# A later second batch of gates in six units, and out_proj's rows added by TensorE in the last unit but one

## The chip, the cores and the metric

The kernel runs on one core of one Trainium2 chip. The metric is the device time of one execution in microseconds; the median of several runs is given. In the profile, PE is TensorE (its matmuls; PEld its weight loads), DVE is VectorE, ACT is ScalarE, POOL is GpSimd and SP is SyncE, which issues the DMAs.

## The reference

The input x has 4 batches of 1024 tokens of 256 channels; all arithmetic is float32. Cut to what matters:

```python
h = layernorm(x)                                         # layer 1: Mamba block, gated MLP
z, xi, B, C, dt_raw = split(rmsnorm(h) @ in_proj.T)      # widths 256, 64, 64, 256, 128
dt = softplus(dt_raw @ dt_proj.T + dt_bias)              # 256 channels, 32 states each
for each token:                                          # the selective scan
    state = exp(dt * A) * state + (dt * xi) * B
    y = sum over states(state * C)
h = h + ((y + xi * D) * silu(z)) @ out_proj.T
hn = rmsnorm(h)
x = x + h + (silu(hn @ gate.T) * (hn @ up.T)) @ down.T   # inner width 704
xn = layernorm(x)                                        # layer 2
out = x + fwht(silu(xn @ W1.T) * (xn @ W3.T)) @ W2.T     # inner width 1024; the kernel folds
                                                         # the Walsh-Hadamard transform into W2
```

## The kernel before

**Units.** The work is cut into eight units, `us[0]` to `us[7]`: four batches by two halves of 512 tokens. A unit's second half starts from the state that its first half left. The scan of a unit runs as 16 steps `q`, 128 in all; one step holds 128 lanes of (channel, state) by 4 blocks by 512 tokens.

**Ticks.** The order of the work on every engine is written out by hand. `at(tick, lane, fn)` puts a piece of work into a list, and a loop at the end of the kernel goes through the ticks, two for each `q`, 256 for the scans, and issues in each tick: lane `PE`, lane `ACT`, the product `times_b` on DVE (L838, tile bx), lane `ACTb` (the copy of B into the PSUM tile pb, L825), the two exps of the next q on ACT (L808), a scan on DVE (L847), lane `DVE`, the second scan, `POOL0`, every second tick the product with C on POOL (`times_c`, L860, in place in da), lane `POOL`, every other tick the sum over states on PE (`sum_states`, L871, into py, after a first matmul with xr and dd, L869, where a half of the unit begins), lanes `PEend`, `ACTend`, SP and the loads. An engine takes its instructions in the order in which they are issued, so the lane and tick of a piece decide behind what it stands. Nothing else plans the order; semaphores between engines are put in by the framework.

**Post-work.** While unit k+1 is scanned, what follows unit k's scan is done in between, from tick E = 32k + 32 on; `post()` puts it into the lists:

- `hr`: the normalized input rows (ACT), and out_proj's product added to them (`add_rows`).
- `row_stats` (ACT, L193 and L196), a few small POOL instructions (`small2`), `hn` (ACT, L226), its transposes (PE, L239) and copies (`ht`, ACT, L246).
- gate and up: `gated()` issues for two batches of three chunks the products pg and pu on PE (L252, two per tick), silus (L289) and ups (L296) on ACT, the products m on POOL (L300). It also carries a half of z of the unit two later (silu at L486). pg and pu are in PSUM tiles of a pool of four, "dense".
- `down`: four row blocks of 128 tokens (`add_rows`, L338), the two copies into hr, `row_stats`, `small3`, `hn`, transposes, `xt`.
- w1 and w3: three batches of `gated()`; then W2's four row blocks, stored at the end.

`add_rows` has three ways to add rows to hr. In way "pe" a matmul with the identity puts hr's rows into PSUM first (L336), the products are added there (L338), and ACT copies the sum back over hr (L352). In way "pool" ACT copies the product out (ev, L360) and POOL adds it (L364). Without a way DVE adds it from PSUM (L348).

The units have three kinds of due times. `many` are units 0 to 5. `us[-2]` is unit 6 (E = 224), whose post-work lies beside the last unit's scans. `last` is unit 7 (E = 256), whose post-work comes after all scans; no scan stands beside it. Half a unit's steps share one pb: its copy is due on ACT at tick E + 15 (and E + 31), and bx of the next tick reads it.

For the prediction's steps in the units 0 to 5: the first batch of gates starts at E + 11, the second at E + 14; the down rows are due at E + 19, 20, 21 and 22 in lane `PE`, that is ahead of the tick's sum over states; yt, the copy of the finished half sum py (L889, ACT), comes at E + 18 or 19, and after it POOL multiplies it by zs (L892). xr·dd of the next half writes py again.

Of the kernel before, what the change touches and what calls it, by code (L numbers as in the profile page):

```python
# [27 lines left out]
def tile_block(ctx: ExitStack, tc: tile.TileContext, a, out):  # L28
# [41 lines left out]
    def dense_psum():  # L70
        return ps_m.tile([P, T], F32, tag="dense", name="dense")
# [148 lines left out]
    def rsqrt_eps(dst, var):  # L220
        nc.gpsimd.tensor_scalar(dst, var, EPS, 1.0, ALU.add, ALU.mult)
        nc.gpsimd.tensor_tensor(dst, dst, mhalf, ALU.pow)

    def scaled_rows(dst, src, scale, bias, ts):
        for t in ts:
            nc.scalar.activation(  # L226
                dst[:, t, :],
                src[:, t, :],
                AF.Identity,
                bias=bias[:, t : t + 1] if bias is not None else 0.0,  # L230
                scale=scale[:, t : t + 1],
            )
# [31 lines left out]
    def at(tick, lane, fn, *args):  # L264
        todo[tick][lane].append(partial(fn, *args))
# [54 lines left out]

            at(tick + 3, "POOL" if three or u is not us[-2] else "POOL0", product, i)

    def add_rows(ticks, u, lhs, rhs, lane="PE", way=None):


        po = {}

        def pe(t):
            if t % 2 == 0:
                po[t // 2] = dense_psum().rearrange("p (t d) -> p t d", t=2)  # L330
            left, right = lhs(), rhs()
            n = len(left)
            dst = po[t // 2][:, t % 2, :]
            if way == "pe":
                rows = u["hr"][:, t, :]
                nc.tensor.matmul(dst, lhsT=ident, rhs=rows, start=True, stop=False)  # L336
            for k in range(n):
                nc.tensor.matmul(  # L338
                    dst,
                    lhsT=left[k][:, t * P : (t + 1) * P],  # L340
                    rhs=right[k],
                    start=(k == 0 and way != "pe"),
                    stop=(k == n - 1),
                )

        def add(i):
            hr = u["hr"][:, 2 * i : 2 * i + 2, :]
            nc.vector.tensor_tensor(hr, hr, po[i], ALU.add)  # L348

        def replace(i):  # L350
            copy = nc.vector.tensor_copy if by_vector(i) else nc.scalar.copy
            copy(u["hr"][:, 2 * i : 2 * i + 2, :], po[i])  # L352

        def by_vector(i):
            return u is us[-1] and i

        def evict(i):
            ev = p3.tile([P, T], F32, tag="up", name="ev")
            po[i] = ev.rearrange("p (t d) -> p t d", t=2), po[i]
            nc.scalar.copy(*po[i])  # L360

        def add_pool(i):
            hr = u["hr"][:, 2 * i : 2 * i + 2, :]
            nc.gpsimd.tensor_tensor(hr, hr, po[i][0], ALU.add)  # L364

        for t in range(TT):
            at(ticks[t], lane, pe, t)
            if t % 2:
                after = ticks[t] + 1
                if way == "pe":  # L370
                    at(after, "DVE" if by_vector(t // 2) else "ACTend", replace, t // 2)
                elif way == "pool":
                    at(after, "ACTend", evict, t // 2)
                    at(after + 1, "POOL", add_pool, t // 2)
                else:
                    at(after, "DVE", add, t // 2)
# [270 lines left out]
    def post(u, E, other):  # L647


        s = {}  # L650
        last = u is us[-1]

        many = us.index(u) < len(us) - 2

        def hr(ts):
            if 0 in ts:
                u["hr"] = p2.tile([P, TT, DM], F32, tag="hr", name="hr")
            scaled_rows(u["hr"], u["x"], u["r1"], u["nm1"], ts)

        def small2():  # L660
            t = sm.tile([P, 2, TT], F32, tag="s2", name="s2")
            r3 = t[:, 1, :]
            rsqrt_eps(r3, u["mv"][:, 1, :])
            s["r3"] = r3

        def small3():
            t = sm.tile([P, 2, TT], F32, tag="s2", name="s2")
            nm, r4 = t[:, 0, :], t[:, 1, :]
            nm16, var = u["mv"][:, 0, :], u["mv"][:, 1, :]
            rsqrt_eps(r4, var)  # L670
            nc.gpsimd.tensor_tensor(nm, nm16, r4, ALU.mult)
            nc.gpsimd.tensor_scalar(nm, nm, 16.0, None, ALU.mult)
            s["r4"], s["nm"] = r4, nm

        def hn(scale, bias):
            s["tok"] = p1.tile([P, TT, DM], F32, tag="tok", name="hn")
            scaled_rows(s["tok"], u["hr"], s[scale], s[bias] if bias else None, range(TT))

        def big(name):
            if last:  # L680

                k = NQ + (1 if name == "m" else 3)
                tiles = [das[i % 5] for i in (k, k + 1)]
                u[name] = [tiles[c // 4][:, c % 4, :] for c in range(8)]
            else:
                tile = p1.tile([P, 8, T], F32, tag="big", name=name)
                u[name] = [tile[:, c, :] for c in range(8)]

        def store(lo=0, n=TT):
            b, first = u["b"], u["c"] * T + lo * P  # L690
            nc.sync.dma_start(
                out=out[b, first : first + n * P, :].rearrange("(t p) d -> p t d", p=P),
                in_=u["hr"][:, lo : lo + n, :],
            )

        at(E + 3, "ACT", hr, (0, 1))
        at(E + 4, "ACT", hr, (2, 3))
        add_rows(
            (E + 3,) * TT,
            u,  # L700
            lambda: [u["yt"][:, k, :] for k in range(2)],
            lambda: [W["wo"][:, k, :] for k in range(2)],
            "PEend",
            way="pool" if many else None,
        )
        for i in range(2):
            at(E + (5 + i if many else 4), "ACTend", row_stats, u, "hr", (2 * i, 2 * i + 1), False)

        F = E + 1 if many else E - 2
        at(E + 7 if many else E + 5, "POOL", small2)  # L710
        at(F + 8, "ACT", hn, "r3", None)
        at(F + 9, "PE", lambda: transposes(u, s["tok"]))
        at(F + 9, "ACTend", transposed, u, "ht")
        at(F + 9, "POOL", lambda: nc.gpsimd.tensor_tensor(u["hr"], u["hr"], u["x"], ALU.add))
        at(F + 10, "PE", big, "m")
        sizes = [min(P, DFF - c * P) for c in range(6)]
        chunks = list(enumerate(sizes))
        for i in range(2):
            gated(F + 10 + 3 * i, u, "m", "wg", "wu", chunks[3 * i : 3 * i + 3], "ht",
                  (other, i) if other else None)  # L720
        down = (18, 19, 20, 21) if many else (17, 17, 18, 18)
        add_rows(
            [F + t for t in down],
            u,
            lambda: [u["m"][c][:n] for c, n in enumerate(sizes)],
            lambda: [W["wd"][:n, c, :] for c, n in enumerate(sizes)],
            way="pe",
        )
        at(F + down[1] + 1, "ACTend", row_stats, u, "hr", (0, 1))
        if last:  # L730
            at(F + down[3] + 1, "DVE", row_stats_vector, u, "hr", (2, 3))
        else:
            at(F + down[3] + 1, "ACTend", row_stats, u, "hr", (2, 3))
        at(F + down[3] + 2, "POOL", small3)
        if not many:
            F -= 3
        at(F + 24, "ACTend" if many else "ACT", hn, "r4", "nm")
        at(F + 25, "PE", lambda: transposes(u, s["tok"]))
        at(F + 25, "ACTend", transposed, u, "xt")
        at(F + 26, "PE", big, "g")  # L740
        chunks8 = [(c, P) for c in range(8)]
        for i in range(3):
            gated(F + 26 + 3 * i, u, "g", "w1", "w3", chunks8[3 * i : 3 * i + 3], "xt")

        o2 = (E + 31, E + 36, E + 50, E + 50) if not (many or last) else range(F + 36, F + 40)
        add_rows(
            o2,
            u,
            lambda: u["g"],
            lambda: [w2h[:, c, :] for c in range(8)],  # L750
            way=None if last else "pool",
        )
        if last:
            at(o2[1] + 1, "SPend", store, 0, 2)
            at(o2[3] + 1, "SPend", store, 2, 2)
        else:
            at(o2[3] + 6, "SPend", store)
# [142 lines left out]
    for k, u in enumerate(us):  # L900
        post(u, 32 * k + 32, us[k + 2] if k + 2 < len(us) else None)
# [148 lines left out]
```

## Time and profile before

| | |
|---|---|
| runs | 1125.77, 1126.01, 1127.81 us; median 1126.01 |
| profiled execution | 1129.06 us, of which the span of the profile is 1127.3 |
| mean granted TensorE clock | 0.925 |
| scans (bx of tick 0 to the last scan's end) | to 1022.8 us of the span |
| bx of tick E + 16, E = 64 / 96 / 128 / 160 / 192 | starts at 335.5 / 459.6 / 582.3 / 707.3 / 831.3 us |

The page cuts the span into 40 slices of 28.2 us; each digit is a tenth of the slice:

```profile
PE   7656246979999799989998999979998999898998
DVE  4899799999989999899999999899989989894000
ACT  3956456887869796888779796979777777584331
POOL 6767668878998899888988899878988788685222
PEclk9777558989999899989999899989999999898999
```

From the ninth slice on, PE and DVE both stand at eight or nine tenths; the last three slices, without DVE, are the post-work of the last unit. `PEclk` is the granted clock; in nearly every unit it loses a tenth or two in one slice.

In the lines of a timeline the columns are start and busy time in us, engine, line, operation, output and inputs, shape, count; in square brackets how long the engine was idle just before, and whom it waited for. In a list of waits the columns are the total, the times and the longest.

### The profile page before, as it was taken

Reading aid. Unit: us, or ns where it says so; the run is one execution under the profiler, and the core shown is the slowest. Engines: PE = TensorE matmul, PEld = TensorE weight load, DVE = VectorE, ACT = ScalarE, POOL = GpSimd, SP = SyncE. Lnnn points to the kernel's source line nnn. Section 1 sums busy time; section 2 is a strip of 40 time slices with the busy share of each in tenths; the row PEclk is TensorE's granted clock in tenths of the full one; section 3 lists DMA queues with packets and bytes.
Section 4 is the critical chain, followed back from the end, with each engine's and each line's share of the span. In section 5 each row is a group of like instructions: output and inputs, shape, how many; then the busy total and the mean of one; then the engine's idle time right before and its main releaser. Section 6 shows DMA issues by size and latency. Waiting matters only on the chain.

```text
span 1127.3 us, 12518 instructions
## 1 busy us (share of the span) xinstructions
PE 980.5 (87%) x3470; PEld 474.4 (42%) x3470; DVE 943.9 (84%) x813; ACT 805.0 (71%) x1443; POOL 882.8 (78%) x512
## 2 busy tenths in 40 slices
PE   7656246979999799989998999979998999898998
PEld 3121012333644345443644354433644363434555
DVE  4899799999989999899999999899989989894000
ACT  3956456887869796888779796979777777584331
POOL 6767668878998899888988899878988788685222
PEclk9777558989999899989999899989999999898999
DMA  7999998998998989998998989899999978760000
GB/s 236 375 363 347 319 377 313 327 317 309 306 342 298 351 302 316 320 333 300 319 347 309 343 284 338 307 337 310 314 321 323 325 255 315 264 223 1 1 19 19
DMA packets 108390, 321.94 MB, mean 286 GB/s; under 512 B 11488, under 2 KB 22176, under 8 KB 108320
## 3 DMA queue, kind: packets, MB, share of 16 engines
q1 hardware_dynamic: 106464, 318.39, 80.8%
q10 hardware_dynamic: 1856, 2.75, 0.7%
q8 instruction: 28, 0.46, 0.2%
q14 instruction: 42, 0.34, 0.1%
HBM read 302.22 MB, written 18.87 MB: 285 GB/s over the span
## 4 chain that ended last, share of the span: by engine, by line
PE 44%; ACT 12%; DMA 7%; DVE 5%; POOL 4%; issue 4%; SPq 0%; DVEq 0%; ACTq 0%; POOLq 0%
PE dense L252 27%; PE dense L338 11%; ACT da L808 5%; DMA da<-dtd 4%; PE py L871 4%; DVE da L847 3%; POOL da L860 3%; DMA ub<-ud 2%; DVE bx L838 2%; ACT up L296 1%; ACT un L226 1%; ACT hr L226 1%; PE dense L336 1%; ACT junk L196 1%; ACT junk L193 1%
## 5 line engine op out<-in xcount | busy, mean ns | idle before, releaser
L860 POOL TENSOR_TENSOR da<-da,cr 128x2048 f32<-128x2048 f32 x128 | 579.2, 4526 | 41.4 <-DVE da L847 19.1
L808 ACT ACTIVATE da<-da,nega 128x512 f32<-128x512 f32 x508 | 335.7, 715 | 72.9 <-DMA da<-dtd 67.3
L838 DVE TENSOR_TENSOR bx<-ub,pb 128x1024 f32<-128x1024 f32 x254 | 312.2, 1229 | 28.5 <-ACT pb L825 11.7
L847 DVE TENSOR_TENSOR_SCAN da<-da,carry,bx 128x512 f32<-128x512 f32 x256 | 313.9, 1267 | 22.0 <-ACT da L808 6.1
L847 DVE TENSOR_TENSOR_SCAN da<-da,bx 128x512 f32<-128x512 f32 x256 | 298.5, 1207 | 17.0 <-DVE bx L838 3.0
L252 PE MATMUL dense<-xt,w 128*128 128x512 f32 x512 | 241.8, 626 | 7.9 <-ACT xt L246 7.9
L871 PE MATMUL py<-da,rsel 128*32 128x512 f32 x1024 | 155.7, 670 | 83.7 <-POOL da L860 83.7
L252 PEld LDWEIGHTS dense<-xt,w 128*128 128x128 f32 x512 | 99.1, 200 | 146.9 <-issue 114.2
L296 ACT COPY up<-dense 128x512 f32<-128x512 f32 x112 | 63.4, 578 | 56.5 <-PE dense L252 56.3
L338 PE MATMUL dense<-w2h,g 128*128 128x256 f32 x448 | 102.1, 383 | 1.2 <-ACT ut L246 1.2
L871 PEld LDWEIGHTS py<-da,rsel 128*32 128x32 f32 x1024 | 23.8, 112 | 179.0 <-POOL da L860 118.4
L338 PEld LDWEIGHTS dense<-w2h,g 128*128 128x128 f32 x448 | 83.5, 190 | 24.2 <-issue 10.4
L300 POOL TENSOR_TENSOR g<-si,up 128x512 f32<-128x512 f32 x56 | 71.0, 1274 | 28.1 <-ACT up L296 28.1
L252 PE MATMUL dense<-ut,win 128*128 128x512 f32 x192 | 92.7, 614 | 0.2 <-ACT ut L246 0.2
L252 PE MATMUL dense<-ht,wg 128*128 128x512 f32 x192 | 87.6, 600 | 3.0 <-ACT ht L246 3.0
L338 PE MATMUL dense<-wd,m 128*128 128x256 f32 x336 | 85.7, 397 | 3.3 <-POOL m L300 3.3
L289 ACT ACTIVATE si<-dense 128x512 f32<-128x512 f32 x112 | 61.9, 595 | 34.9 <-PE dense L252 34.5
L252 PE MATMUL dense<-ht,wu 128*128 128x512 f32 x160 | 73.9, 601 | 1.8 <-ACT si L289 1.8
L300 POOL TENSOR_TENSOR m<-si,up 128x512 f32<-128x512 f32 (+1 forms) x42 | 52.6, 1274 | 26.1 <-ACT up L296 26.1
L338 PEld LDWEIGHTS dense<-wd,m 128*128 128x128 f32 x336 | 63.2, 195 | 21.2 <-issue 9.3
L808 ACT ACT_TABLE_LOAD x46 | 59.0, 1283 | 0.8
L252 PEld LDWEIGHTS dense<-ut,win 128*128 128x128 f32 x192 | 36.8, 197 | 52.5 <-issue 41.0
(110 smaller groups left out, 884.4 us busy)
## 6 DMA issues: line engine op xcount, KB each, us to landing
da<-dtd SPq DMA_DIRECT2D x254, 512.0 KB
ub<-ud SPq DMA_DIRECT2D x254, 512.0 KB
cr<-cd SPq DMA_DIRECT2D x64, 256.0 KB
x<-in_x SPq DMA_DIRECT2D x8, 512.0 KB
dtd<-dt SPq DMA_DIRECT2D x16, 256.0 KB
ud<-du SPq DMA_DIRECT2D x16, 256.0 KB
cd<-cc SPq DMA_DIRECT2D x16, 256.0 KB
xr<-xbd SPq DMA_DIRECT2D x60, 64.0 KB
```

The lines of the kernel that those rows point to most:

```text
L193: nc.scalar.activation(junk, src[:, t, :], AF.Identity, scale=-1.0 / (16 * DM), accum_out=nm)
L226: nc.scalar.activation(dst[:, t, :], src[:, t, :], AF.Identity, bias=bias[:, t : t + 1] if bias is not None else 0.0, scale=scale[:, t : t ...
L252: nc.tensor.matmul(dst[:n], lhsT=w[:, k, col : col + n], rhs=src[:, k, :], start=(k == 0), stop=(k == 1),)
L289: nc.scalar.activation(g[i]["si"][:n], g[i]["pg"][:n], AF.Silu)
L296: nc.scalar.copy(g[i]["up"][:n], g[i]["pu"][:n])
L300: nc.gpsimd.tensor_tensor(u[dst][c][:n], g[i]["si"][:n], g[i]["up"][:n], ALU.mult)
L338: nc.tensor.matmul(dst, lhsT=left[k][:, t * P : (t + 1) * P], rhs=right[k], start=(k == 0 and way != "pe"), stop=(k == n - 1),)
L808: nc.scalar.activation(da, da if q else s["u"]["pdt", b], AF.Exp, scale=an[:, s["h"], s["j"], b, s["g"] : s["g"] + 1],)
L838: nc.vector.tensor_tensor(s["bx"], s["ub", b0 // 2], u["pb"].unsqueeze(1).broadcast_to([P, 2, T]), ALU.mult)
L847: nc.vector.tensor_tensor_scan(da, da, s["bx"][:, b % 2, :], start, ALU.mult, ALU.add)
L860: eng.tensor_tensor(da, da, s["cr"].unsqueeze(1).broadcast_to([P, n, T]), ALU.mult)
L871: nc.tensor.matmul(u["py"][32 * b : 32 * b + 32, :], lhsT=rsel[:, 2 * s["j"] + s["g"], :], rhs=s["da"][:, b, :], start=False, stop=last,)
```

## The change

For the six `many` units:

- the second batch of gates starts at E + 15 instead of E + 14;
- the down rows are due at E + 20, 21, 21, 22 in lane `PEend` (behind the tick's sum over states) instead of E + 19, 20, 21, 22 in lane `PE`;
- the copy of the first two row blocks into hr, and their statistics, come at E + 22 instead of E + 21; those of the last two stay at E + 23, and so does all that follows.

For `us[-2]`:

- all hr rows are made at E + 3; out_proj's rows are added in way "pe" (four identity matmuls, two copies on ACT) instead of by two adds on DVE; the statistics are at E + 4 and E + 5, small2 at E + 6;
- hn, ht, hr + x, gates and down come a tick later than before (gates at E + 9 and E + 12, down at E + 16, 16, 17, 17), the copies into hr, the statistics and small3 two ticks later (copies at E + 18 and E + 19, small3 at E + 20), and hn, xt and the w1/w3 batches two ticks later (E + 21, 22, and 23, 26, 29);
- W2's row blocks are at E + 36, 36, 50, 50 instead of 31, 36, 50, 50, so that all four stand behind the scans, which end at E + 32.

For `last` nothing changes. SP's instructions keep their order. On PE in the `many` units the pieces between pu of the first batch and the last down row stand as follows (sum n is the sum over states of tick E + n):

```
before: pg3 pg4 pg5 z | sum15 | pu3 pu4 c | sum17 | down0 | xr·dd sum19 | dt | down1 down2 | sum21 | c | down3 | sum23
after:  pg3 pg4 | sum15 | pg5 z c pu3 pu4 | sum17 | xr·dd sum19 | dt | down0 | sum21 | down1 down2 | c | down3 | sum23
```

On POOL the second batch's products m move behind the product with C of tick E + 18; on ACT the exps of tick E + 16 move ahead of the second batch's silus.

The diff, with the `add_rows` signature and its copies first:

```diff
-    def add_rows(ticks, u, lhs, rhs, lane="PE", way=None):
+    def add_rows(ticks, u, lhs, rhs, lane="PE", way=None, extra=0):
...
-                after = ticks[t] + 1
+                after = ticks[t] + 1 + extra
...
-        at(E + 4, "ACT", hr, (2, 3))
+        at(E + 4 if many else E + 3, "ACT", hr, (2, 3))
...
-            way="pool" if many else None,
+            way="pool" if many else None if last else "pe",
...
-            at(E + (5 + i if many else 4), "ACTend", row_stats, u, "hr", (2 * i, 2 * i + 1), False)
-
-        F = E + 1 if many else E - 2
-        at(E + 7 if many else E + 5, "POOL", small2)
+            at(E + (5 + i if many else 4 if last else 4 + i), "ACTend", row_stats, u, "hr", (2 * i, 2 * i + 1), False)
+
+        F = E + 1 if many else E - 2 if last else E - 1
+        at(E + 7 if many else E + 5 if last else E + 6, "POOL", small2)
...
-            gated(F + 10 + 3 * i, u, "m", "wg", "wu", chunks[3 * i : 3 * i + 3], "ht",
+            gated(F + 10 + (4 if many else 3) * i, u, "m", "wg", "wu", chunks[3 * i : 3 * i + 3], "ht",
...
-        down = (18, 19, 20, 21) if many else (17, 17, 18, 18)
+        extra = int(not (many or last))
+        down = (19, 20, 20, 21) if many else (17, 17, 18, 18)
...
+            "PEend" if many else "PE",
             way="pe",
+            extra=extra,
         )
-        at(F + down[1] + 1, "ACTend", row_stats, u, "hr", (0, 1))
+        at(F + down[1] + 1 + extra, "ACTend", row_stats, u, "hr", (0, 1))
...
-            at(F + down[3] + 1, "ACTend", row_stats, u, "hr", (2, 3))
-        at(F + down[3] + 2, "POOL", small3)
+            at(F + down[3] + 1 + extra, "ACTend", row_stats, u, "hr", (2, 3))
+        at(F + down[3] + 2 + extra, "POOL", small3)
         if not many:
-            F -= 3
+            F -= 3 - extra
...
-        o2 = (E + 31, E + 36, E + 50, E + 50) if not (many or last) else range(F + 36, F + 40)
+        o2 = (E + 36, E + 36, E + 50, E + 50) if not (many or last) else range(F + 36, F + 40)
```

## The prediction

> **What bounds the kernel now.** First the page's busy lines, then the waits by total, then VectorE (DVE) tick by tick, then TensorE (PE) around one unit's join.
>
> ```profile
> PE 980.5 (87%) x3470; PEld 474.4 (42%) x3470; DVE 943.9 (84%) x813; ACT 805.0 (71%) x1443; POOL 882.8 (78%) x512
> DVE bx L838 <- ACT pb L825: 11.7, 6, 3.5
> ```
>
> PE and DVE are both near full. DVE sets the tick: one bx of 1.23 and two scans of 1.2 to 1.27 make 3.7 to 3.9 us, 256 times. What DVE loses in the loop is therefore lost time. The second line (total, times, longest) is one such loss: bx of tick E+16 waits for the copy of B. By unit E=64 to 192 it is 3.48, 2.17, 1.51, 1.80 and 2.44 us. I follow E=128:
>
> ```profile
> 577.92 1.98 PE L252 MATMUL dense<-ht,wu 128*128 128x512 f32 x4
> 580.00 0.59 ACT L296 COPY up<-dense 128x512 f32<-128x512 f32 x1 [2.20 <-PE dense L252]
> 581.72 0.58 ACT L825 COPY pb<-br 128x512 f32<-128x512 f32 x1
> 582.33 1.23 DVE L838 TENSOR_TENSOR bx<-ub,pb 128x1024 f32<-128x1024 f32 x1 [1.51 <-ACT pb L825]
> ```
>
> Read upwards: bx waits for pb, which stands in ScalarE's (ACT's) queue behind the copy of up2, which waits 2.20 us for PE. So PE is late. How it came to be late shows in the windows after the unit's joins (columns: us, PE busy, granted clock, DMA share, GB/s):
>
> ```profile
> 617.50:620.90 3.40, 1.06 (x8) 1.00 0.82 290
> 620.90:631.20 10.30, 8.83 (x15) 0.50 1.02 396
> 631.20:707.00 75.80, 74.80 (x278) 1.00 0.93 315
> ```
>
> From 631.2 to 707.0, that is from the w1 gates to the next unit's tick E+16, PE is busy 74.80 of 75.80 us: whatever starts this stretch later makes the next bx at E+16 later, one for one. The stretch starts when the last down row (down3, ends 615.2) has been copied, its statistics taken, and hn made and transposed. **The many-unit cycle is TensorE's**: pu2, down3, hn, w1 gates, next pu2.
>
> **Units 0 to 5: what moves.** All that PE does up to pu2 keeps its order, so the stall at E+16 is not taken away at its source. Behind pu2 the orders are
>
> before: pg3 pg4 pg5 z, sum15, pu3 pu4 c, sum17, **down0**, xr·dd, sum19, dt, down1 down2, sum21, c, down3;
> after: pg3 pg4, sum15, pg5 z c pu3 pu4, sum17, xr·dd, sum19, dt, **down0**, sum21, down1 down2, c, down3.
>
> ```profile
> 593.04 1.06 PE L871 MATMUL py<-da,rsel 128*32 128x512 f32 x8
> 594.58 2.95 PE L338 MATMUL dense<-wd,m 128*128 128x256 f32 x12
> 597.45 1.12 PE L869 MATMUL py<-xr,dd 128*128 128x512 f32 x2
> 599.45 1.16 PE L871 MATMUL py<-da,rsel 128*32 128x512 f32 x8 [0.87 <-POOL da L860]
> 612.33 2.95 PE L338 MATMUL dense<-wd,m 128*128 128x256 f32 x12
> 595.66 0.57 ACT L889 COPY yt<-py 128x512 f32<-128x512 f32 x1
> 590.60 1.27 POOL L300 TENSOR_TENSOR m<-si,up 128x512 f32<-128x512 f32 x1 [3.68 <-ACT up L296]
> 594.87 4.53 POOL L860 TENSOR_TENSOR da<-da,cr 128x2048 f32<-128x2048 f32 x1
> ```
>
> Before, down0 (594.04 with its ident matmuls, to 597.45) fills the time in which ACT gets to the yt copy; xr·dd writes the PSUM tile that this copy reads. After, xr·dd comes first and waits. The added wait: sum17 still ends at 594.04 (the same instructions stand ahead of it, in another order), yt ends near 596.2 (ACT's work ahead of it, ups, cc and exps, is the same): 2.2 us. Queued behind it on PE: sum19, dt and every down row. Bounds of this wait from the rows: nothing, if ACT comes to yt 2.2 us earlier; 5.1 us, the longest PE wait on yt anywhere in the trace (unit 0). I take 2.2, worked out in place.
>
> Then, with row-to-row times: xr·dd 1.12 to 597.3, sum19 1.09 to 598.4, dt 1.82 to 600.2, down0 3.41 to 603.6. sum21 needs POOL's da of tick E+20. POOL after: da18 moves ahead of the products into POOL's idle 3.68 us: from 589.7 (its scans end) 4.8 with the carry copy to 594.5, three m of 1.27 to 598.3, yt·zs 1.28 to 599.6, da20 4.8 to 604.4. So sum21 waits 0.8 and ends 605.4; down1 and down2 6.72, c 1.82, down3 3.31: 617.25, against 615.21. In waits: 2.2 + 0.8 − 0.87 (sum19 waits no more), so **+2.0 us** for down3.
>
> What hides it: after down3 come copy (0.59), statistics (2.4), exps, hn. The exps of tick E+26 wait 1.24, 0.59 and 0.94 us for DMA in E=64, 128, 160, and a late ACT uses these up; E=96 and 192 have no such cover. The w1 gates move by 1.3 (E=32, where PE waits 4.53 for POOL at 246.3 anyway), 0.75, 2.05, 1.5, 1.05, 2.0: **+8.7 us**.
>
> At nothing: the first hr copy and its statistics a tick later (ACT is idle 1.24 before the second copy at 615.32; without that cover at most their 0.59 + 2.4); SP's queue, which keeps its order, so that transfers wait for the same or earlier sums (sum19 599.4 to 597.3, sum21 609.1 to 604.4), with a gain of at most the 0.57 us that the scan at 606.46 waits for its exp.
>
> **The granted clock.** In the row 617.50 PE is busy 31% of 3.4 us, and the next 10.3 us run at 0.50; windows with 48% or more kept 1.00. A new wait of 2.2 us inside one such stretch leaves some 35%, across two of them over half. So about half of the six units may fall, each losing 0.7 (one stretch, 0.8 of it covered by sum21's wait) to 2.4 us. Bounds 0 to 6 × 2.4 = +14; I take **+1.5**, as the rows right after (sum19, dt, down0) are the ones slowed, and one stretch busy over 88% brings the clock back.
>
> The Trainium skill, "TensorE: Matmul & The Clock Gate", section "HAM oscillation — how this bites in real kernels", speaks of no PE-idle gaps over about 3.4 us. By it a wait of 2.2 us would cost no clock, and the sum would be 1.5 us lower. The trace differs: a single wait of 2.69 us at 621.25, after 1.12 us of waiting, lies in the stretch that cost half the clock.
>
> **Unit 6 (E=224) and the tail.**
>
> ```profile
> 911.51 0.69 DVE L348 TENSOR_TENSOR hr<-hr,dense 128x512 f32<-128x512 f32 x1 [2.66 <-PE dense L338]
> 913.24 0.69 DVE L348 TENSOR_TENSOR hr<-hr,dense 128x512 f32<-128x512 f32 x1 [1.04 <-PE dense L338]
> 977.63 2.45 DVE L847 TENSOR_TENSOR_SCAN da<-da,carry,bx 128x512 f32<-128x512 f32 x2 [2.87 <-ACT da L808]
> 966.23 0.59 ACT L352 COPY hr<-dense 128x512 f32<-128x512 f32 x1 [8.38 <-PE dense L338]
> 1036.88 0.59 ACT L360 COPY ev<-dense 128x512 f32<-128x512 f32 x1 [1.61 <-PE dense L338]
> ```
>
> The two adds and their waits leave DVE: 2.66 + 0.69 + 1.04 + 0.69 = 5.1 us. The copies L352, which hold the exps behind them (8.38 us, then the scan's 2.87 and 0.38), come two ticks later, after their rows: 3.25 us. DVE gains 8.3. What is late next is PE: it takes on four ident matmuls (0.54 each by their starts, 2.2) and drops one W2 block (3.6) from the loop. Its own waits to the end go: 3.72 at 978.73, 2.30 and 1.30 for the last sums. −3.7 − 2.3 − 1.3 − 3.6 + 2.2 = −8.7 at best for the last sum (ends 1028.8 before); with 1.1 us of new waits for silu and ups at E+13, −7.6. The W2 block then stands in the tail between out_proj and hn of the last unit, as the present one does (1033.17 to 1036.8, its ev on ACT ahead of hn): +3.6. Net −5.1 to −4.0; bounds by rows: −8.3 if PE hides the block, and +2.2 if DVE's gain turns wholly into waits for PE while the four matmuls stay. I take **−4.7**.
>
> **Sum.** +8.7 + 1.5 − 4.7 = +5.5. The profiled execution took 1129.06 (span 1127.3), 3 us above the median of 1126.0; on that, 1131.5, on the profile 1134.5. I predict 1131.
>
> **The rivals.**
> A, forecast: the TensorE cycle is longer by the yt wait, 1130 to 1133. For: 74.80 of 75.80. Chance 0.53.
> B, faster: ACT reaches yt early, or POOL's earlier da pays back what PE waits (POOL loses its 3.68 us of idleness), so that the six units cost under 0.4 us each, and the eight us of DVE stalls in unit 6 decide: −4.7, 1121. For: POOL stands in PE's waits on sums (0.87, and 1.12 at 617.40). Against: those sums are before down3 only in part. It decides from less than 0.4 us a unit. Chance 0.21.
> C, balance: the DMA waits at E+26 hide more, 0.8 us a unit: 1126. Chance 0.13.
> D, clock: every unit's wait of 2.2 us costs a stretch at half clock, 1.5 us more in each: 1126 + 8.7 − 4.7 + 9 = 1139. Chance 0.13.
>
> **The numbers.** Within 0.2% (2.25 us, about what a measurement here tells from no change) is C; faster is B; slower A and D: 0.21, 0.13, 0.66. The range runs from 1119 (B with the unit-6 bound halfway) to 1139 (the middle of D); outside lie about half of D and a third of B's low side. The likeliest case alone is 1128 to 1134.
>
> **What would show it.** Right: PE waits of about 2.2 us at xr·dd on yt in each of six units; bx on pb from 11.7 to about 20; down3 ending 34.9 us after bx of E+16 instead of 32.9; unit 6's DVE adds and the 2.87 gone; two W2 blocks ahead of the last hn. Wrong: yt copied before sum17 ends; the pb wait at or below 11.7; new DVE waits in unit 6 over 3 us; a DMA wait that ends a tick where ACT did.

## The result, and the profile after

The changed kernel takes 1139.66 us (median of four runs, 1137.17 to 1140.95); the kernel before, 1126.91 in the same set (1125.77 to 1130.58). The ratio is 1.0105, 95% interval 1.0073 to 1.0137: slower by 8 to 15 us. The forecast was +5, to 1131, with a range to 1139: the sign is right, and the loss is a little over twice the forecast. In microseconds the median lies just above that range; the ratio on the 1126.0 from which the forecast started gives 1137.8. The profiled execution is the fastest of the four (1137.17, span 1135.4), 8.1 us above the profiled one of before, while the medians lie 12.8 apart: the two traces show some two thirds of the loss.

Where the time is: the start of bx (us of the span) at a few ticks, from the two traces.

| tick | before | after | difference |
|---|---|---|---|
| 64 (first of the third unit) | 272.3 | 272.8 | +0.5 |
| 128 | 521.1 | 522.7 | +1.6 |
| 160 | 642.4 | 648.5 | +6.1 |
| 224 (first of the last unit) | 890.8 | 901.0 | +10.2 |
| 255 (last) | 1019.0 | 1023.6 | +4.6 |
| transposes of the last unit's hn | 1037.9 | 1046.0 | +8.1 |

So the six units lost 10.2 us, unit 6 gave back 5.7 in the loop, and the tail took 3.5 again. TensorE's (PE's) timeline of the same unit as in the prediction (E = 128; bx of E + 16 now starts at 587.17; line numbers are three higher than before):

```profile
597.88 1.06 PE L874 MATMUL py<-da,rsel 128*32 128x512 f32 x8
601.60 1.92 PE L872 MATMUL py<-xr,dd 128*128 128x512 f32 x2 [2.66 <-ACT yt L892]
603.45 1.92 PE L874 MATMUL py<-da,rsel 128*32 128x512 f32 x8
605.29 1.98 PE L447 MATMUL dense<-raw,dtw 128*128 128x512 f32 x4
607.55 2.95 PE L338 MATMUL dense<-wd,m 128*128 128x256 f32 x12
...
610.42 1.06 PE L874 MATMUL py<-da,rsel 128*32 128x512 f32 x8
...
620.50 2.95 PE L338 MATMUL dense<-wd,m 128*128 128x256 f32 x12
...
629.41 2.80 PE L239 MATMUL dense<-ident,hn 128*128 128x128 f32 x8 [4.11 <-ACT hn L226]
```

The wait that was forecast is there: after sum17, xr·dd waits 2.66 us for ScalarE's (ACT's) copy yt. The next two rows take 1.92 us each, where the same work took 1.12 and 1.16 before: they run at half clock. sum21 (610.42) does not wait. The last down row ends at 623.45. The windows of the same unit (columns: us, PE busy, granted clock, DMA share, GB/s) say the same:

```profile
598.40:601.80 3.40, 0.74 (x9) 1.00 0.91 345
601.80:605.20 3.40, 3.40 (x10) 0.50 0.75 263
605.20:623.50 18.30, 18.30 (x80) 1.00 0.84 290
...
629.10:635.90 6.80, 6.07 (x12) 0.50 1.02 399
635.90:713.40 77.50, 76.50 (x282) 1.00 0.93 315
```

A stretch of 3.4 us in which PE is busy 22% is followed by 3.4 us at clock 0.50, in which PE is busy throughout. The rows are cut where the clock can change: in every trace here the changes lie whole multiples of 3.41 us apart, so that a stretch at 0.50 lasts 3.41, 6.83, 10.24 or 13.65 us, or longer by such steps. The second stretch at 0.50, behind the wait for hn, was in the kernel before as well. All six units wait 2.65 or 2.66 us for yt at E + 19, and each has its stretch.

On VectorE (DVE), the wait of bx for pb (11.7 us in 6 waits before) is hardly longer; scans wait for exps at other ticks instead:

```profile
DVE bx L841 <- ACT pb L828: 14.2, 8, 3.5
DVE da L850 <- ACT da L811: 16.5, 27, 2.3
```

The second row was 7.9 us before. In the unit shown, 1.50 us of it is at E + 26, behind the late copy of the down rows and its statistics on ACT. DVE's waits for the DMA of ub, 11.0 us in all before, are 11.0 after: the loss is not there.

How the loss runs through the units can be read from three times in each, measured from its own bx of E + 16: the end of down3, the start of the w1 gates, and from there the way to the next unit's bx of E + 16.

| kernel | down3 ends (E = 64 to 192) | w1 gates start | from w1 to the next bx of E + 16 (E = 32 to 160) |
|---|---|---|---|
| before | 32.7 to 33.0 | 41.9 to 43.5 | 80.7 to 82.2 |
| after | 36.1 to 36.3 | 45.2 to 45.4 | 80.2 to 80.9 |

The last column is PE's stretch without waits and hardly depends on the kernel: on average 81.3 before and 80.6 after. Down3 ends some 3.3 us later, the gates start 2.7 later on average, and with the shorter last column 2.2 us of it arrive at the next unit's E + 16: from E = 64 to 192 the four cycles take 504.5 us instead of 495.7.

### The profile page after: what moved, and what is told of

The parts are those of the page before. It is cut to its first block, busy times and chain, and to the rows that moved or that the text cites. A ratio compares the mean times of both kernels' runs of the same rounds, so it can differ in the third digit from the quotient of the medians.

```text
span 1135.4 us, 12536 instructions
## 1 busy us (share of the span) xinstructions
PE 985.0 (87%) x3478; PEld 474.1 (42%) x3478; DVE 943.9 (83%) x811; ACT 805.1 (71%) x1443; POOL 882.0 (78%) x512
## 3 DMA queue, kind: packets, MB, share of 16 engines
q1 hardware_dynamic: 106464, 318.39, 80.7%
q10 hardware_dynamic: 1856, 2.75, 0.7%
## 4 chain that ended last, share of the span: by engine, by line
PE 57%; ACT 13%; DMA 13%; POOL 8%; issue 4%; DVE 4%; SPq 0%; DVEq 0%; POOLq 0%; ACTq 0%
PE dense L252 33%; PE dense L338 14%; PE py L874 6%; POOL da L863 6%; ACT da L811 5%; DMA da<-dtd 5%; DMA ub<-ud 3%; DVE da L850 2%; DVE bx L841 1%; ACT hn L226 1%; PE dense L336 1%; ACT up L296 1%; PE py L872 1%; PE dense L447 1%; DMA br<-xbd 1%
## 5 line engine op out<-in xcount | busy, mean ns | idle before, releaser
L841 DVE TENSOR_TENSOR bx<-ub,pb 128x1024 f32<-128x1024 f32 x254 | 312.1, 1229 | 29.9 <-ACT pb L828 14.2
L338 PE MATMUL dense<-wd,m 128*128 128x256 f32 x336 | 82.5, 387 | 0.0
```

The lines of the kernel that those rows point to most:

```text
L338: nc.tensor.matmul(dst, lhsT=left[k][:, t * P : (t + 1) * P], rhs=right[k], start=(k == 0 and way != "pe"), stop=(k == n - 1),)
L841: nc.vector.tensor_tensor(s["bx"], s["ub", b0 // 2], u["pb"].unsqueeze(1).broadcast_to([P, 2, T]), ALU.mult)
```

## The experiments

Theory 1: the order on PE makes the wait for yt, the wait brings half clock, and both lengthen PE's cycle. Rival 2: unit 6 and the tail make the loss. Rival 3: the later gates with their later products make it, in whatever queue. Ratios are against the kernel before, run on the same chip; its median was 1128.1 to 1129.0 us in these sets.

**The six units alone** (`six_only`). Edit: all lines of the diff for unit 6 undone.

```diff
-            way="pool" if many else None if last else "pe",
+            way="pool" if many else None,
...
-        F = E + 1 if many else E - 2 if last else E - 1
+        F = E + 1 if many else E - 2
...
-        extra = int(not (many or last))
+        extra = 0
...
-        o2 = (E + 36, E + 36, E + 50, E + 50) if not (many or last) else range(F + 36, F + 40)
+        o2 = (E + 31, E + 36, E + 50, E + 50) if not (many or last) else range(F + 36, F + 40)
```

> Against the kernel before. The six units' part alone, unit 6 as before. Theory 1 (in each of the six units TensorE waits 2.7 us for the copy yt because xr·dd now stands ahead of down0, and the wait costs a stretch of 3.4 us at half clock; both lengthen TensorE's cycle): +10 us (9 to 12), scans of tick 224 some 10 us later than before. Rival 2 (unit 6 and its W2 block in the tail make the loss): under +5 us.

Measured: 1142.83 us, ratio 1.0131 (1.011 to 1.0152), 12 to 17 us. Down3 ends at 36.2 to 36.3, as in the changed kernel, and each unit has the 2.66 us wait and the 3.4 us at half clock. Tick 224 starts 13.2 us later than before, of which 2.0 were there at tick 48, with which the first of the six units only begins to differ. A little more than theory 1 said; rival 2 falls.

**Unit 6 alone** (`unit6_only`). Edit: the lines for the six units undone.

```diff
-            gated(F + 10 + (4 if many else 3) * i, u, "m", "wg", "wu", chunks[3 * i : 3 * i + 3], "ht",
+            gated(F + 10 + 3 * i, u, "m", "wg", "wu", chunks[3 * i : 3 * i + 3], "ht",
...
-        down = (19, 20, 20, 21) if many else (17, 17, 18, 18)
+        down = (18, 19, 20, 21) if many else (17, 17, 18, 18)
...
-            "PEend" if many else "PE",
```

> Against the kernel before. Unit 6's part alone, the six units as before. Theory 1: -2 us (-4 to 0): the loop gains 5.5 us, the second W2 block ahead of the last unit's hn takes 3.5 back. Rival 2: +3 us or more.

Measured: 1124.35 us, ratio 0.9963 (0.9949 to 0.9977), 2.6 to 5.8 us faster. In the trace the loop gains 6.2 us from tick 224 to the end, and from the last scan's end to the transposes of the last hn it takes 18.7 instead of 15.2: PE's W2 rows there take 7.07 us instead of 3.62, which is the second block, 3.5 us. The two parts of the change add up to it: 1.0131 times 0.9963 is 1.0094.

**dt ahead of xr·dd** (`dt_first`): the two dt matmuls as a filler in the wait.

```diff
-        at(H - 13, "PEend", pe_dt)
+        at(H - 13, "PE", pe_dt)
```

> The changed kernel, with the two dt matmuls (1.8 us) moved ahead of xr·dd in the six units, into the wait. Theory 1: the wait falls from 2.7 to 0.9 us, no stretch at half clock follows, down3 ends some 33 us after bx of E+16 instead of 36.3; the time falls from +12 to between -1 and +4 us against before. Rival 3 (the later second batch of gates and its later products cost the time, by whatever queue, and the wait is harmless): stays at +10 or more.

Measured: 1141.45 us, ratio 1.012 (1.0103 to 1.0137). The expectation of theory 1 failed, and the time is one that rival 3 gave. PE's timeline of the unit E = 128 shows why:

```profile
605.20 1.98 PE L447 MATMUL dense<-raw,dtw 128*128 128x512 f32 x4
607.93 1.12 PE L872 MATMUL py<-xr,dd 128*128 128x512 f32 x2 [0.75 <-ACT yt L892]
...
610.52 2.95 PE L338 MATMUL dense<-wd,m 128*128 128x256 f32 x12
615.43 1.16 PE L874 MATMUL py<-da,rsel 128*32 128x512 f32 x8 [1.97 <-POOL da L863]
```

The wait for yt shrinks to 0.75, and sum21 now waits 1.97 for GpSimd (POOL): 2.72 together, as much as before. POOL's product of E + 20 ends at 615.4 behind the product of E + 18, the three late m and yt·zs. So there are two gates one behind the other, and three of the four down rows now stand behind the second one. The sum21 wait brings half clock in four of the five units 64 to 192 (not in this one), and down3 ends at 35.1 to 36.7.

**dt twice** (`dt_twice`): the dt matmuls issued once ahead of xr·dd, without use, and again at their place.

```diff
-        def pe_dt(hs=(0, 1)):
-            if 0 in hs:
+        def pe_dt(hs=(0, 1), new=True):
+            if 0 in hs and new:
                 s["pv"] = {}
             for h in hs:
-                s["pv"][h] = dense_psum()
+                if new:
+                    s["pv"][h] = dense_psum()
...
-        at(H - 13, "PEend", pe_dt)
+        at(H - 13, "PE", pe_dt)
+        at(H - 13, "PEend", pe_dt, (0, 1), False)
```

> The changed kernel with the two dt matmuls issued twice in the six units: once ahead of xr·dd, with no use, and again at their place. TensorE is busy in 1.8 us of the wait, but nothing that follows starts earlier for it. Theory 1 with both parts: the stretch at half clock goes, the wait's delay stays: down3 34.5 us after bx of E+16, +5 to +8 us against before. If the clock alone made the loss: -1 to +3. If the clock costs nothing: +11 or more.

Measured: 1133.62 us, ratio 1.0052 (1.0036 to 1.0069). More work on PE, and 7.8 us less than `dt_first`, on the same chip. PE in the unit E = 128:

```profile
599.59 1.98 PE L448 MATMUL dense<-raw,dtw 128*128 128x512 f32 x4
602.32 1.13 PE L874 MATMUL py<-xr,dd 128*128 128x512 f32 x2 [0.75 <-ACT yt L894]
603.37 1.06 PE L876 MATMUL py<-da,rsel 128*32 128x512 f32 x8
604.37 1.98 PE L448 MATMUL dense<-raw,dtw 128*128 128x512 f32 x4
...
609.81 1.16 PE L876 MATMUL py<-da,rsel 128*32 128x512 f32 x8 [0.24 <-POOL da L865]
```

xr·dd and sum19 take 1.1 again, and none of the units 64 to 192 has a stretch at half clock there. Down3 ends at 34.8 to 35.1. The time is what theory 1 gave with both parts. Down3's delay thus splits: 3.3 us in the changed kernel, of which 1.3 are clock and 2.0 the order. In time, 1.0105 against 1.0052 makes about 6 us for the clock, by the intervals some 2 to 10.

**The later down rows alone** (`down_only`) and **the later gates alone** (`gates_only`), unit 6 as before in both.

```diff
-        down = (18, 19, 20, 21) if many else (17, 17, 18, 18)
+        down = (19, 20, 20, 21) if many else (17, 17, 18, 18)
...
+            "PEend" if many else "PE",
```

> The kernel before with the later down rows alone (E+20, 21, 21, 22, behind the tick's sum); gates and unit 6 as before. Theory 1, as the runs so far leave it (down0 no longer fills the time up to the copy yt, and the rows stand behind sum21, which waits for POOL; the waits bring half clock): w1 gates 44 to 45.5 us after bx of E+16 instead of 42.6; +6 to +10 us. Rival 3 (the later gates make the loss): within 2 us of before.

Measured: 1155.03 us, ratio 1.0246 (1.0226 to 1.0266). The direction of theory 1, but three times its size. PE in the unit E = 128 (bx of E + 16 at 593.40):

```profile
604.11 1.06 PE L874 MATMUL py<-da,rsel 128*32 128x512 f32 x8
607.35 2.07 PE L872 MATMUL py<-xr,dd 128*128 128x512 f32 x2 [2.18 <-ACT yt L892]
610.52 2.03 PE L874 MATMUL py<-da,rsel 128*32 128x512 f32 x8 [1.09 <-POOL da L863]
612.48 2.78 PE L447 MATMUL dense<-raw,dtw 128*128 128x512 f32 x4
```

Here the three m still stand ahead of POOL's product of E + 18, so sum19 waits as well (1.09 to 2.03 us by unit), and the half clock lasts 6.8 us instead of 3.4. The w1 gates start at 47.2 to 48.0. The expectation had left out this second wait.

```diff
-            gated(F + 10 + 3 * i, u, "m", "wg", "wu", chunks[3 * i : 3 * i + 3], "ht",
+            gated(F + 10 + (4 if many else 3) * i, u, "m", "wg", "wu", chunks[3 * i : 3 * i + 3], "ht",
```

> The kernel before with the later second batch of gates alone; down rows and unit 6 as before. Theory 1: down0 waits for the products of the second batch, which POOL makes behind da of E+18, about 1.5 us; down3 ends 33.6 us after bx of E+16 (32.9 before): +1 to +5 us, the upper end if the wait brings half clock. Rival 3: +8 or more.

Measured: 1133.86 us, ratio 1.005 (1.0035 to 1.0066). In the unit E = 128 down0 waits twice 0.53 us for m; in the units 64 to 192 no new stretch at half clock follows, and down3 ends at 33.4. In the unit E = 32 down0 waits 2.75 us for m, 6.8 us at 0.50 follow, and down3 ends at 35.8 instead of 29.9. Rival 3 (8 us or more) falls, though the later gates alone cost some 6 us (4 to 7), a little more than theory 1 gave. Beside the later down rows they save: they take POOL's m out of sum19's way, and the ratio is 1.0131 (`six_only`) instead of 1.0246.

**Useless matmuls in the wait for hn** (`warm4`), in the kernel before; and the same beside unit 6's part (`unit6_warm4`).

```diff
+    def warm(u, n):
+        u["pt"] = [dense_psum() for _ in range(2)]
+        for _ in range(n):
+            nc.tensor.matmul(
+                u["pt"][0], lhsT=ident, rhs=W["w1"][:, 0, :T], start=True, stop=True
+            )
...
+        if many:
+            at(F + 24, "PEend", warm, u, 4)
-        at(F + 25, "PE", lambda: transposes(u, s["tok"]))
+        at(F + 25, "PE", lambda: transposes(u, s["tok"], many))
```

With the last argument, `transposes` writes into the tiles that `warm` took.

> The kernel before with four matmuls of no use (identity by 512 columns of W1, 1.8 us in all) in each of the six units, issued after the sum of E+25, into the PSUM tile of the next transposes, so that TensorE is busy in part of its wait for hn. If the granted clock falls for that wait and costs TensorE's cycle 3 to 4 us a unit, as 6.8 to 10.2 us at 0.5 in each unit suggest: the stretches at half clock after E+26 go, the stalls of bx on pb (11.7 us) go to near zero, -7 to -12 us. If the clock there costs nothing: 0 to +2 us.

> Unit 6's part of the change and the four matmuls of no use together, the six units otherwise as before. If both gains stand in different places: -11 to -17 us against before.

Measured: `warm4` 1122.16 us, ratio 0.9947 (0.9928 to 0.9965); `unit6_warm4` 1117.82 us, 0.9913 (0.9897 to 0.9928). Faster, though both by somewhat less than expected. The four took 3.70 us, twice the 1.8 expected, and just about fit: in the unit E = 128 the transposes of hn start 39.7 us after bx of E + 16 instead of 38.9, and end at 41.2 instead of 41.7. PE there:

```profile
613.43 1.16 PE L881 MATMUL py<-da,rsel 128*32 128x512 f32 x8 [1.09 <-POOL da L870]
614.52 3.70 PE L247 MATMUL dense<-w,ident 128*128 128x512 f32 x8
618.06 0.56 PE L240 MATMUL dense<-ident,hn 128*128 128x128 f32 x3
618.78 0.77 PE L240 MATMUL dense<-ident,hn 128*128 128x128 f32 x5 [0.16 <-ACT hn L226]
620.69 3.70 PE L260 MATMUL dense<-xt,w 128*128 128x512 f32 x8 [1.14 <-ACT xt L254]
```

The first eight gate rows take 3.70 where they took 6.69 at half clock in the kernel before:

```profile
625.12 6.69 PE L252 MATMUL dense<-xt,w 128*128 128x512 f32 x8 [1.07 <-ACT xt L246]
```

The clock row of the page, before (shown in the section on the profile before) and in `warm4`:

```profile
PEclk9777558989999999999999999999999999898999
```

The dips of the units E = 64 to 192 are gone from the row, and in the trace one stretch of 3.4 us behind hn is left of theirs (736.9); the unit E = 32 keeps 6.8 us of 13.7. The stalls of bx on pb at E + 16 are 1.61, 0.73, 0.58, none and 0.65 us instead of 3.48, 2.17, 1.51, 1.80 and 2.44.

**The changed kernel with such matmuls** (`after_warm6`): the same edit, six of them.

> The changed kernel with six useless matmuls (2.7 us) in each of the six units after the sum of E+25, where TensorE waits 4.1 us for hn. Theory 1: the wait for yt and its stretch at half clock stay (down3 still 36.3 us after bx of E+16), but the 6.8 us at half clock after hn go: the w1 gates come earlier or run faster, some 2 to 3 us a unit; 0 to +4 us against before instead of +12. If the loss of the change had nothing to do with TensorE's clock: +10 or more.

Measured: 1129.26 us, ratio 1.0006 (0.9992 to 1.002), as theory 1 said; the way from the w1 gates to the next bx falls from 80.8 to 79.2 us. One part was not as expected: all six units still wait 2.65 or 2.66 us for yt, but only three of them, E = 64, 128 and 160, have the half clock after it. There down3 ends at 36.1 to 36.3; in E = 96 and 192 it ends at 34.8 and 35.0. The windows at the clock's steps, of E = 64 and then of E = 96:

```profile
349.00:352.40 3.40, 0.75 (x8) 0.99 0.88 305
352.40:355.80 3.40, 3.39 (x10) 0.50 0.98 311
...
471.80:475.20 3.40, 2.50 (x12) 1.00 0.90 327
475.20:478.60 3.40, 1.65 (x10) 1.00 0.90 310
478.60:482.00 3.40, 3.40 (x18) 1.00 0.92 264
```

In E = 64 the wait lies in one step, which is left 22% busy; in E = 96 it is spread over two, 74% and 49% busy, and the clock stays. So it is not the length of the wait alone that decides, but how it falls on the steps. Within one kernel this also gives the clock's price in down3 once more: 1.1 to 1.5 us.

**Unit 6 taken apart**: `unit6_pe` adds out_proj's rows by TensorE, for which two hr rows are made a tick earlier, and leaves all other ticks; `unit6_ticks` makes all the rest and leaves the adds to DVE.

```diff
-        at(E + 4, "ACT", hr, (2, 3))
+        at(E + 4 if many or last else E + 3, "ACT", hr, (2, 3))
...
-            way="pool" if many else None,
+            way="pool" if many else None if last else "pe",
```

> The kernel before with one thing of unit 6 changed: out_proj's rows added by TensorE (way pe, hr made at E+3), all ticks as before, W2's block in the loop. If the two adds and their waits on DVE (5.1 us) are a gain of their own: -2 to -5 us. If ACT's copies, which now wait for the same rows in front of the exps, give it back: within 1 us.

> The kernel before with the rest of unit 6's part: everything from its statistics on later, W2's second block in the tail, but out_proj's rows still added by DVE. The scan's 3.2 us at E+20 and 21 go, the block costs 3.5 in the tail: -1 to +2 us. Together with the run of way pe this should add up to unit 6's part, -4.6 us.

Measured: `unit6_pe` 1.0018 (1.0004 to 1.0031), `unit6_ticks` 0.9993 (0.9982 to 1.0004); together, as in `unit6_only`, 0.9963. They do not add up. In `unit6_pe` DVE has no adds and no wait at E + 4, and then:

```profile
941.63 2.45 DVE L847 TENSOR_TENSOR_SCAN da<-da,carry,bx 128x512 f32<-128x512 f32 x2 [3.36 <-ACT da L808]
954.32 1.28 DVE L847 TENSOR_TENSOR_SCAN da<-da,carry,bx 128x512 f32<-128x512 f32 x1 [1.26 <-ACT da L808]
```

DVE is earlier, but the exps that it needs are not. ACT's copy of the added rows waits 2.00 us for PE, and the silus and ups behind it, which stand ahead of exps and wait 0.91 to 1.12 us each for PE as in the kernel before, come 1.8 us later than there. At E + 12 and 15 DVE has caught up with them, and its wait at E + 20 is 4.10 us instead of 2.87. Without the later ticks the adds' removal is given back.

**Unit 6 kept busy too** (`unit6_warm_all`): as `unit6_warm4`, and in unit 6

```diff
+        elif not last:
+            at(F + 24, "PE", warm, u, 6)
```

> Unit 6's part and the four useless matmuls in the six units (9 to 10 us faster than before so far), and six more (2.7 us) ahead of the sum of E+21 in unit 6, where TensorE waits 3.7 us for POOL and the clock is 0.5 for the 10.2 us that follow. If unit 6's end is TensorE's: 2 to 5 us less than without them, -11 to -15 against before. If the scans or POOL end it: no more than 1 us.

Measured: 1116.00 us, ratio 0.9892 (0.9877 to 0.9907), the fastest kernel here. Against `unit6_warm4` (0.9913, in another set) the intervals overlap; the last unit's hn is transposed at 1025.0 in its trace against 1024.1. The ratio lies in the range expected of a gain, but a gain from these six is not shown.

## Why the prediction was right or wrong

The direction and the terms for the order and for unit 6 came out. The step that failed is the clock's: forecast at +1.5 us, it measures about 6.

- **"The many-unit cycle is TensorE's."** Right: from the w1 gates to the next bx of E + 16 it takes 80 to 82 us in every order tried (79.2 where the matmuls of no use hold the clock), and of what the join loses most arrives: some 2.2 of 3.3 us a unit.
- **"All that PE does up to pu2 keeps its order, so the stall at E + 16 is not taken away."** Right. That the lost time would show there (11.7 to about 20 us) was wrong: it was 14.2, the rest fell on exps at E + 4, 5 and 26. The tick at which DVE waits is not fixed.
- **The wait for yt, 2.2 us.** Right in place, 2.66 in size: the two late ups are copied later (ACT waits 1.13 us for PE before them), and yt starts 13.8 instead of 13.3 us after bx of E + 16. Without the later gates (`down_only`) it starts at 13.3, and the wait is 2.18.
- **sum21 waits 0.8 for POOL.** Covered in the changed kernel, where the half clock puts PE behind POOL; without half clock it is 0.24 (`dt_twice`) or, with the first wait filled, 1.97 (`dt_first`).
- **+2.0 us for down3 by the order.** Right in sum, with some luck in its parts: `dt_twice`, without the half clock, has 34.8 to 35.1 where 34.9 was forecast, but as 2.66 + 0.24 − 0.87 and not as 2.2 + 0.8 − 0.87. The list by units came out too: in E = 64 to 192 the w1 gates of `dt_twice` start 0.75, 2.12, 1.41, 1.10 and 2.09 us later than before, where 0.75, 2.05, 1.5, 1.05 and 2.0 were forecast. (E = 32 is an exception: 3.8 against 1.3, with a wait of 2.94 for POOL and half clock behind it.) 1.0052 over unit 6's 0.9963 is about +10 us for the six units against +8.7.
- **"About half of the six units may fall … I take +1.5."** This is the term that was mis-sized. The clock measures about 6 us (1.0105 against 1.0052), 1.3 us a unit in down3. Its idea was sound: whether a wait costs clock depends on how it falls on the steps, and in `after_warm6`, with the same wait, three of six fell. In the changed kernel it lay in one step in every unit, which left 22 to 34% busy, and all six fell; from E = 64 on its units come 125.8 to 126.2 us apart, close to 37 steps, so the wait meets the steps in nearly the same way each time. That the units would fall alike was not considered. Besides, the 1.5 was less than the forecast's own figures gave: three units at 0.7 to 2.4 us are 2.1 to 7.2. D, in which every unit falls and which was given 0.13, is the case that came.
- **"One stretch busy over 88% brings the clock back."** It did so behind the wait for yt, but the trace of before has a case against it in unit 6: from 958.9 to 962.3 PE is busy throughout at 0.50, and the clock stays at 0.50 for another 3.4 us.
- **Unit 6 and tail, −4.7.** Right: −2.6 to −5.8 alone. The tail's +3.6 is 3.5; the new DVE wait at E + 13, forecast 1.1 us, is 1.58 alone and 2.30 in the changed kernel. That the adds' 5.1 us are won only together with the later copies was not seen.
- **The Trainium skill**, "TensorE: Matmul & The Clock Gate", "HAM oscillation — how this bites in real kernels", names idle gaps over about 3.4 us. The runs agree with the trace of before against it: a wait of 2.66 us brought half clock in each of the six units, and waits of 1.73 to 1.95 us, after 0.75 a little earlier, in four of five in `dt_first`.

What stays open: why the units of the changed kernel settle at a distance of 37 steps, and what share of a step has to be busy. That the six units cost 10.2 us in the changed kernel's trace and 13.2 in that of `six_only` is no more than single executions leave open: 2.0 of the 13.2 were there at tick 48, and the executions of one kernel spread over 3 to 7 us.

## What to carry to other kernels

Before a piece of work is moved out from between two others, ask what the engine did with that time: down0 looked early, but it filled TensorE's wait for a copy, and behind it stood a second gate on another engine, so that filling only the first won nothing. On the engine that closes the cycle, price a new wait twice, once as time and once as clock, by the busy share around it. If the units all have the same length, do not count on half of them escaping: the wait can fall alike in each. Try useless matmuls there: they tell the two apart, and here they won 0.5% by themselves. A removed stall is won only if the engine that takes the work over has room at that tick.

## What the runs showed of the hardware

In the 14 traces of this case the granted clock is 1.00 or 0.50, and its changes lie whole multiples of 3.41 us apart. What a step's busy share does can be read at the waits for yt and POOL. In the changed kernel steps busy 22 to 34% were followed by 0.50. In `after_warm6` 22, 29 and 42% were, while 47 and 49% were not. In `dt_first` waits of 1.73 to 1.95 us left 43 to 50% and were followed by 0.50; one of 1.97 us left 55% and was not. So here the border lies near half, and a wait well under 3.41 us is enough. It is not exact: in `gates_only` a step with 2.30 of 3.40 us busy (1038.0), most of it transposes, was followed by 0.50 too.

In the changed kernel bx of E + 16 comes 125.8, 126.2, 126.2 and 126.2 us after that of the unit before (E = 96 to 192); its stretches at 0.50 behind the wait begin 126.3 apart, which is 37 steps. The kernel's cycle seems to have locked to the clock's steps; that was seen, and not tried. In the kernel before the distances are 122.7 to 125.0.
